# Layer 1's second half by pairs of tiles, with ScalarE's statistics and b1 added by transfers

## The chip, the cores and the metric

The kernel runs on one core of a Trainium2 chip. The metric is device time in microseconds (us) of one execution; lower is better. The engines work at the same time, each through its own queue in order: TensorE (PE: matmuls, with its weight loads as PEld), VectorE (DVE), ScalarE (ACT), GpSimd (POOL) and SyncE (SP). In this kernel POOL and SP issue the transfers (DMA).

## The reference, cut to what matters

Four graph layers follow each other on 2708 nodes with 512 features, all float32 and with the same dense adjacency matrix `adj`. Each layer normalizes x, keeps what is positive, and adds a graph convolution to x. The change is in the second layer, "layer 1":

```python
def _L1_gnn_ref(x, adj, W, b):
    deg = adj.sum(axis=1)
    dis = (deg + EPS) ** (-0.5)
    a_norm = dis[:, None] * adj * dis[None, :]
    h = a_norm @ x
    return h @ W.T + b

# --- layer 0 (adj_preln) ---
h = jnp.maximum(_layernorm(x, axis=-1), 0.0)
x = x + _L0_gnn_ref(h, adj, L0_gnn_weight)      # ends in relu, no bias
# --- layer 1 (adj_preln) ---
h = jnp.maximum(_layernorm(x, axis=-1), 0.0)
x = x + _L1_gnn_ref(h, adj, L1_gnn_W, L1_gnn_b)
# --- layers 2 and 3 in the same way; layer 3 is an attention layer with gates ---
```

`_layernorm` takes mean and variance over the 512 features of each node.

## The kernel before, in words

The 2708 nodes are kept as 20 full tiles of 128 nodes (0 to 19) and two tail tiles, 20 and 21, which hold the nodes left over in each quarter of the matrix. `h` is the normalized input of a layer and stays in SBUF. x itself lives in DRAM, one block of 128x512 a tile, named `xs0` to `xs21`.

A layer has two parts. The aggregation (`aggregate`, for layer 0 `first_aggregate`) multiplies `adj` with `h` by a scheme that needs seven block products in place of eight, twice nested: seven outer steps, each with two column pieces `u` of seven inner products. `multiply` writes one such piece: its products `pa`, `pb`, `pc`, `pd` are each five matmuls of 128x339 columns (L541), ScalarE copies `v` from `pa` (L575), and VectorE joins them (L581 makes `u2`, L588 `u3`, then L557 to L564 add to the sum `agg`). Before a piece, VectorE makes sums of matrix blocks (L512 to L516) that SP's transfers (L445, L447) brought into the seven places of `obuf`. A place becomes free again when the piece is done, so the transfers of a piece wait for the piece before.

The epilogue (`next_x`) multiplies `agg` with the layer's weight and makes the next x and h. It runs in two halves: the first (`H1`, tiles 0 to 9) after outer step 5, the second (`H2`, tiles 10 to 21) after outer step 3, the layer's last. For each tile: POOL loads the tile of x (L916), TensorE does four matmuls of 512 columns with the tile's columns of `agg` as weights (L203), VectorE scales the product and adds b1 (L931), adds it to x (L934), POOL stores x (L935), and VectorE takes mean and variance with bn_stats and bn_aggr (L234, L235). After three tiles, a chain of small instructions makes the scale and the shift (L239, ScalarE's square root L224, L225 to L230, L940, L247), and ScalarE writes the three tiles of `h` (L255). Tail tiles need their columns gathered first (L181), and tile 21 also takes two steps on TensorE (L206 and L210) with a copy by ScalarE between them (L208). In layers 0 and 2 ScalarE scales and cuts off the product (L929) in place of L931.

The same saving scheme with seven products exists for two tiles at once: `pair_product`, with `sums_of_pair` for the tiles and `weights_of_pairs` for the weight. Before, layer 3's gates use it (L1077 for its matmuls, of 257 columns), and layer 3's attention.

A scheduler orders the instructions of each engine: it follows the program's order, but moves ahead what it finds ready, so parts of neighbouring stages lie among each other. POOL's queue holds the loads and stores of x, the loads of the weights (`load_w`, L156) and the accumulating transfers of layer 0 (L744); a transfer that waits holds up those behind it.

Of the kernel before, what the change touches and what calls it, by code (L numbers as in the profile page):

```python
# [8 lines left out]
FP = mybir.dt.float32  # L9
AF = mybir.ActivationFunctionType  # L10
ALU = mybir.AluOpType

P = 128
D = 512
NC = D // P
# [3 lines left out]
KT = Q // P  # L19
# [3 lines left out]
W = (Q + 1) // U  # L23
NF = NQ * KT
# [13 lines left out]
def gnn_kernel(  # L38
# [20 lines left out]
    nc = tc.nc  # L59
# [5 lines left out]
    upool = ctx.enter_context(tc.tile_pool(name="upool", bufs=1))  # L65
    ytp = ctx.enter_context(tc.tile_pool(name="ytp", bufs=1))
    small = ctx.enter_context(tc.tile_pool(name="small", bufs=2))
    dram = ctx.enter_context(tc.tile_pool(name="dram", bufs=1, space=bass.MemoryType.DRAM))
    ps_agg = ctx.enter_context(tc.tile_pool(name="ps_agg", bufs=5, space=bass.MemoryType.PSUM))
# [23 lines left out]
    dinv = dd[:, 1]  # L93
# [52 lines left out]
    def take(places):  # L146

        places.append(places.pop(0))
        return places[-1]

    def new_y():
        return take(y_places)
# [6 lines left out]
    def full_cols(a, t):  # L159
        k = t % KT  # L160
        return a[..., k * P : (k + 1) * P]
# [75 lines left out]
    def rstd_of(mv, n):  # L237
        v = small_cols("rv", n)
        nc.vector.tensor_scalar(v[:, :n], mv[:, :n, 1], LN_EPS, None, ALU.add)  # L239
        rstd = small_cols("rstd", n)  # L240
        rsqrt(rstd[:, :n], v[:, :n], n)
        return rstd

    def shift_of(mv, scale, n, at=None):

        b = small_cols("sh", n)
        last = nc.vector.scalar_tensor_tensor(  # L247
            b[:, :n], mv[:, :n, 0], -1.0, scale[:, :n], ALU.mult, ALU.mult
        )
        if at is not None:  # L250
            at.append(last.ins)
        return b

    def normalized(t, src, scale, shift, fs=slice(0, D)):
        nc.scalar.activation(h[:, t, fs], src[:, fs], AF.Relu, bias=shift, scale=scale)  # L255
# [279 lines left out]
    def bank(name):  # L535
        return ps_agg.tile([P, W], FP, tag="agg", name=name)
# [131 lines left out]
    def aggregate(self_loops, epilogue, hooks=None):  # L668


        def outer(p, *dests):
            outer_product(p, self_loops, *dests)
            if hooks is not None and p in hooks:
                hooks[p]()

        outer(1, (0, 0, "as it is"))
        first_part_of_both()
        by_halves(nc.vector.tensor_sub, XA, XA, XB)
        outer(7, (1, 1, "as it is"))
        nc.vector.tensor_sub(XB, XB, XD)  # L680
        outer(2, (0, 0, "added"))
        minus_sum(XA, XD, XA)
        nc.vector.tensor_add(XC, XC, XA)
        outer(4, (1, 0, "as it is"))
        tails(self_loops, (0, 1))
        outer(6, (0, 1, "added"))
        ends_of_sums()
        outer(5, (0, 1, "less"), (1, 1, "less"))
        tails(self_loops, (2, 3))
        epilogue(H1)  # L690
        outer(3, (0, 1, "added"))
        epilogue(H2)
# [215 lines left out]
        epilogue(H2)  # L908


    def project(w_sb, t):
        return tile_product(t, tile_cols(agg, t), [w_sb[:, c, :] for c in range(NC)])

    def load_x(t, src):
        xt = take(xt_places)
        nc.gpsimd.dma_start(xt, src[t])  # L916
        return xt

    def next_x(ts, w_sb, scale, bias, src, colscale, after=None):
        for g in groups(ts):  # L920
            n, t0 = len(g), g[0]
            mv = small.tile([P, KT, 2], FP, tag="mv", name="mv")
            xts = []
            for s, t in enumerate(g):
                xt = load_x(t, src)
                po = project(w_sb, t)
                y = new_y()
                if bias is None:
                    nc.scalar.activation(y, po, AF.Relu, scale=scale[:, t : t + 1])  # L929
                else:  # L930
                    nc.vector.scalar_tensor_tensor(  # L931
                        y, po, scale[:, t : t + 1], bias, ALU.mult, ALU.add
                    )
                nc.vector.tensor_add(xt, xt, y)  # L934
                nc.gpsimd.dma_start(xs[t], xt)  # L935
                stats(xt, mv[:, s, :])
                xts.append(xt)
            rstd = rstd_of(mv, n)
            if colscale is not None:
                nc.vector.tensor_mul(rstd[:, :n], rstd[:, :n], colscale[:, t0 : t0 + n])  # L940
            sh = shift_of(mv, rstd, n)
            for s, t in enumerate(g):
                normalized(t, xts[s], rstd[:, s : s + 1], sh[:, s : s + 1])
                if after is not None:
                    after(t)
# [5 lines left out]
    w_sb = []  # L951

    def first_epilogue(ts):
        if not w_sb:
            w_sb.append(load_w(w0))
        next_x(ts, w_sb[0], dinv, None, x, dis)

    first_aggregate(first_epilogue)


    w1_sb = load_w(w1)
    b1_bc = misc[:, 0:D]
    nc.gpsimd.dma_start(b1_bc, b1.partition_broadcast(P))
    aggregate(False, lambda ts: next_x(ts, w1_sb, dis, b1_bc, xs, dinv))


    def broadcast_columns(po, cs):
# [54 lines left out]
    def make_vs():  # L1022
# [2 lines left out]

    aggregate(
        True,
        lambda ts: next_x(ts, w2_sb, dinv, None, xs, None, keep_h),
        {2: make_vs, 3: lambda: h_dots((5, 6))},
    )  # L1030

# [9 lines left out]
            wg_sb[:, :, k, D // 2 :], wab[0:D, k : k + 1].rearrange("(c p) o -> p c o", p=P)  # L1041
        )

    def in_four(a):
        return a.rearrange("p (k c o) -> p k c o", k=4, c=NC // 2)

    def weights_of_pairs(w, sums):

        w11, w12, w21, w22 = (w[:, f : f + 2, k] for f in (0, 2) for k in range(2))
        t1, t2, t3, t4 = sums
        nc.vector.tensor_sub(t1, w12, w11)
        nc.vector.tensor_sub(t2, w22, t1)
        nc.vector.tensor_sub(t3, w22, w12)
        nc.vector.tensor_sub(t4, w21, t2)
        return {1: w11, 2: w21, 3: w22, 4: t4, 5: t1, 6: t2, 7: t3}

    def sums_of_pair(ts, places):
        (a11, a12), (a21, a22) = (  # L1060
            [full_cols(agg[:, f, t // KT // 2, :, t // KT % 2], t) for f in range(2)] for t in ts
        )
        sums_ = take(places)
        s1, s2, s3, s4 = (sums_[:, k] for k in range(4))
        nc.vector.tensor_sub(s3, a11, a21)
        nc.vector.tensor_add(s1, a21, a22)
        nc.vector.tensor_sub(s2, a22, s3)
        nc.vector.tensor_sub(s4, a12, s2)
        return {1: a11, 2: a12, 3: s4, 4: a22, 5: s1, 6: s2, 7: s3}

    def pair_product(xs_, ws, bank, first_block_last=False):

        n = ws[1].shape[-1]

        def part(ps, k, start):
            for c in range(2):
                nc.tensor.matmul(  # L1077
                    ps, xs_[k][:, c], ws[k][:, c], start=start and c == 0, stop=c == 1,
                    skip_group_check=not start,
                )  # L1080

        def place(tag, bufs=1):
            return upool.tile([P, W], FP, tag=tag, name=tag, bufs=bufs)[:, 0:n]

        pa = bank("pa", n)
        part(pa, 1, True)
        v = place("v")
        nc.scalar.copy(v, pa)
        pb = bank("pb", n)
        part(pb, 6, True)  # L1090
        u2 = place("u2", 2)
        nc.vector.tensor_add(u2, v, pb)
        yield
        if not first_block_last:
            part(pa, 2, False)
        pc = bank("pc", n)
        part(pc, 7, True)
        u3 = place("u3")
        nc.vector.tensor_add(u3, u2, pc)
        yield  # L1100
        pd = bank("pd", n)
        part(pd, 5, True)
        c22 = place("s")
        nc.vector.tensor_add(c22, u3, pd)
        yield
        part(pc, 4, False)
        c21 = u3
        nc.vector.tensor_add(c21, u2, pc)
        part(pd, 3, False)
        c12 = u2  # L1110
        nc.vector.tensor_add(c12, u2, pd)
        if first_block_last:
            part(pa, 2, False)
        yield [[pa, c12], [c21, c22]]

    def gates_bank(name, n):
        pool, tag = (ps_out, "out") if name == "pb" else (ps_agg, "agg")
        return pool.tile([P, n], FP, tag=tag, name=name)

    both_places = ends[:, NC * D + 2 * NC :]  # L1120
    wg_sums = in_four(both_places[:, 0 : 4 * NC // 2 * GW])
    wg_sums = [wg_sums[:, k] for k in range(4)]
    s_places = [
        in_four(both_places[:, o : o + 4 * NC // 2 * P])
        for o in (4 * NC // 2 * GW, 4 * NC // 2 * (GW + P))
# [109 lines left out]
    def place(t):  # L1235

        if t < NF:
            o = (t // KT) * Q + (t % KT) * P
            return [(0, P, o)]
        if t == NF:  # L1240
            return [(q * R0, R0, q * Q + KT * P) for q in range(NQ)]
        return [(q * R1P + PAD, R1, q * Q + KT * P + R0) for q in range(NQ)]
# [231 lines left out]
```

## Time and profile before

| what | value |
| --- | --- |
| median of three runs | 2073.58 us (2071.27 to 2076.43) |
| the profiled execution, its own time | 2070.74 us |
| its span, first to last instruction | 2069.0 us, clock granted to TensorE 0.998 |
| VectorE, busy share | 72% |
| ScalarE, busy share | 20% |
| share of the chain of waits: TensorE, VectorE, DMA | 83%, 7%, 5% |
| layer 0's second epilogue, start on TensorE | 411.18 us |
| layer 1's first epilogue, start on TensorE | 717.36 us |
| layer 1's second epilogue, start on TensorE | 791.73 us |

A timeline line gives the start in us, the length, the engine, the line of the kernel, the operation with output and inputs, the shape and the number of instructions merged into it. One float32 matmul is two records. Records of matmuls overlap in the timeline, so what a matmul costs is read from one start to the next. In brackets stands the idle time ahead of the instruction and what ended it.

### The profile page before, as it was taken

The page shows a single profiled execution, that of the slowest core. Times are in us where ns is not written, and L with a number is a line of the kernel's source. Part 1 is how long each engine was busy: PE and PEld are TensorE (multiplying, and loading weights), DVE is VectorE, ACT ScalarE, POOL GpSimd, SP SyncE. Part 2 cuts the span into 40 slices and gives each one's busy share as a digit, 9 for nine tenths or more (in the row PEclk, how much of TensorE's full clock was granted, in tenths as well). Part 3 has the DMA queues.
Part 4 walks back from the last instruction along what each step waited for, and adds up shares of the span by engine and source line. Part 5 has one row for each costly group of instructions (what it writes and reads, how often), then busy time and mean ns, then how long its engine had stood idle before and what let it go on. Part 6 is the DMA issues. An engine that isn't in the chain of part 4 may idle for free.

```text
span 2069.0 us, 20285 instructions
## 1 busy us (share of the span) xinstructions
PE 2028.0 (98%) x7330; PEld 1282.2 (62%) x7330; DVE 1495.6 (72%) x2592; ACT 406.2 (20%) x822; POOL 198.8 (10%) x361
## 2 busy tenths in 40 slices
PE   5999999999999999999999999999999999999998
PEld 2566655646666655666664646666677666676666
DVE  4678877756777777766587889967758866677644
ACT  1430001130000010100002130000026444444411
POOL 0111111120000011100002130001001000001011
PEclk9999999999999999999999999999999999999999
DMA  9998595555545444754454565545543332323231
GB/s 369 305 378 265 180 338 187 190 186 179 174 154 176 146 168 142 239 178 161 161 170 144 204 208 188 171 156 186 185 147 121 112 105 95 110 88 123 87 100 52
DMA packets 81476, 363.69 MB, mean 176 GB/s; under 512 B 11568, under 2 KB 16876, under 8 KB 81248
## 3 DMA queue, kind: packets, MB, share of 16 engines
q1 hardware_dynamic: 51104, 245.95, 34.7%
q0 software_dynamic: 30272, 116.45, 17.4%
q8 instruction: 58, 0.95, 0.2%
q14 instruction: 42, 0.34, 0.0%
HBM read 297.39 MB, written 62.19 MB: 174 GB/s over the span
## 4 chain that ended last, share of the span: by engine, by line
PE 83%; DVE 7%; DMA 5%; issue 4%; POOL 1%; ACT 0%; SPq 0%; POOLq 0%; DVEq 0%; ACTq 0%
PE pe L1364 17%; PE pc L541 13%; PE pa L541 13%; PE pd L541 13%; PE po L203 8%; PE pb L541 7%; PE pt L603 3%; DMA obuf<-in_yb_dram 3%; PE pd L1077 1%; PE pc L1077 1%; PE pa L1077 1%; PE pt L608 1%; PE pe L603 1%; DMA osumt<-ends 1%; DVE ends L1004 1%
## 5 line engine op out<-in xcount | busy, mean ns | idle before, releaser
L1364 PE MATMUL pe<-obuf,h 128*128 128x339 f32 x1280 | 373.2, 448 | 0.0
L541 PE MATMUL pa<-obuf,h 128*128 128x339 f32 x1040 | 317.0, 449 | 2.5 <-ACT h L255 1.4
L1364 PEld LDWEIGHTS pe<-obuf,h 128*128 128x128 f32 x1280 | 241.4, 189 | 121.8 <-issue 4.1
L541 PEld LDWEIGHTS pa<-obuf,h 128*128 128x128 f32 x1040 | 195.2, 189 | 109.5 <-issue 9.2
L203 PE MATMUL po<-ends,agg 128*128 128x512 f32 x480 | 207.5, 593 | 0.0
L1228 ACT ACTIVATE e<-r,nsr 128x339 f32<-128x339 f32 x352 | 172.4, 566 | 178.5 <-DVE obuf L1232 86.4
L541 PE MATMUL pb<-t,s 128*128 128x339 f32 x560 | 170.9, 451 | 1.8 <-DVE s L473 1.0
L541 PE MATMUL pc<-t,h 128*128 128x339 f32 x560 | 169.5, 448 | 1.5 <-DVE u L588 1.5
L541 PE MATMUL pd<-t,s 128*128 128x339 f32 x560 | 169.0, 447 | 0.0
L541 PE MATMUL pd<-obuf,s 128*128 128x339 f32 x550 | 166.3, 448 | 0.2 <-DVE agg L562 0.2
L575 ACT COPY v<-pa 128x339 f32<-128x339 f32 x56 | 24.6, 439 | 718.2 <-PE pa L541 691.3
L203 PEld LDWEIGHTS po<-ends,agg 128*128 128x128 f32 x480 | 90.9, 190 | 114.3 <-issue 109.3
L541 PEld LDWEIGHTS pb<-t,s 128*128 128x128 f32 x560 | 106.3, 191 | 57.3 <-DVE t L513 2.1
L541 PEld LDWEIGHTS pc<-t,h 128*128 128x128 f32 x560 | 105.7, 189 | 56.8 <-DVE u L588 3.1
L541 PEld LDWEIGHTS pd<-t,s 128*128 128x128 f32 x560 | 105.8, 189 | 54.1
L541 PEld LDWEIGHTS pd<-obuf,s 128*128 128x128 f32 x550 | 104.0, 189 | 53.9 <-DVE agg L562 1.3
L541 PE MATMUL pc<-obuf,s 128*128 128x339 f32 x450 | 135.9, 448 | 0.0
L541 PEld LDWEIGHTS pc<-obuf,s 128*128 128x128 f32 x450 | 85.1, 189 | 43.8 <-issue 0.5
L935 POOL DMA_DIRECT2D xs<-ends x66 | 35.9, 544 | 780.6 <-DVE ends L934 705.4
L513 DVE TENSOR_TENSOR t<-obuf,t 128x1695 f32<-128x1695 f32 x55 | 105.3, 1915 | 0.0
L1232 DVE SCALAR_TENSOR_TENSOR obuf<-obuf,e 128x1695 f32<-128x1695 f32 x32 | 61.5, 1923 | 57.9 <-DMA obuf<-in_yb_dram 40.7
L514 DVE TENSOR_TENSOR t<-obuf,t 128x1695 f32<-128x1695 f32 x52 | 99.5, 1914 | 0.1
(321 smaller groups left out, 2415.4 us busy)
## 6 DMA issues: line engine op xcount, KB each, us to landing
obuf<-in_yb_dram SPq DMA_DIRECT2D x132, 847.5 KB, 4.5
obuf<-osumt SPq DMA_DIRECT2D x100, 847.5 KB, 4.5
osumt<-obuf POOLq DMA_DIRECT2D x22, 847.5 KB, 12.2
xs<-ends POOLq DMA_DIRECT2D x66, 256.0 KB, 2.3
ends<-xs POOLq DMA_DIRECT2D x60, 256.0 KB, 4.2
obuf<-in_yt_dram SPq DMA_DIRECT2D x28, 339.0 KB, 3.6
obuf<-in_yb_dram POOLq DMA_DIRECT2D x11, 847.5 KB, 11.0
ends<-in_yb_dram SPq DMA_DIRECT2D x9, 847.5 KB, 9.2
```

Of the source, the lines that this page charges most:

```text
L203: nc.tensor.matmul(po, cs[c], ws[c], start=(c == 0), stop=(c == NC - 1))
L513: nc.vector.tensor_add(t2, o22, t1)
L514: at_y.append(nc.vector.tensor_add(t4, o21, t2).ins)
L541: last = nc.tensor.matmul(ps, x[:, k, :], y[:, k, :], start=start and k == 0, stop=k == KT - 1, skip_group_check=not start,)
L575: at_v.append(nc.scalar.copy(v, pa).ins)
L603: nc.tensor.matmul(ps[c], h[:, NF, c * P : (c + 1) * P], tl[:, 0, :], start=start, stop=False)
L608: nc.tensor.matmul(ps[c], h[g, NF + 1, c * P : (c + 1) * P], tl[g, 1, :], start=False, stop=True)
L935: nc.gpsimd.dma_start(xs[t], xt)
L1077: nc.tensor.matmul(ps, xs_[k][:, c], ws[k][:, c], start=start and c == 0, stop=c == 1, skip_group_check=not start,)
L1228: nc.scalar.activation(e[:, k], row, AF.Exp, bias=nsr[:, t, s : s + 1], scale=1.0)
L1232: nc.vector.scalar_tensor_tensor(b, b, 0.0, e1[:, :n], ALU.not_equal, ALU.min)
L1364: nc.tensor.matmul(pe[c], h[:, t, c * P : (c + 1) * P], a, start=(t == 0), stop=False)
```

## The change

1. In layer 1 alone, the second half (tiles 10 to 21) is done by `next_x_by_pairs`: first the tail tiles 20 and 21 as before by `next_x`, then tiles 10 to 19 as five pairs by `pair_product`, each with seven products of two matmuls of 256 columns.
2. In those pairs, mean and variance come from ScalarE (`stats_by_act`): a sum, a scaling, a sum of squared differences and another scaling, in place of bn_stats and bn_aggr.
3. b1 is no longer added in the epilogue. While layer 0 and layer 1 run, 22 accumulating transfers on POOL's queue add it to the kept x in DRAM, one a tile (`add_b1`). They are handed over after outer steps 7, 2, 4 and 6 of layer 1; the scheduler may place them earlier, and in the built order they stand among layer 0's stores of x. In layer 1 the scaled product is added to x in one VectorE instruction, in both halves.
4. The pairs need room: the sums of the weight take two quarters of `misc` (where b1 lay) and part of one of the seven places of `obuf`, which is borrowed until the last pair is done; the sums of the tiles take the tail tile's place `yt` and the rest of that block. The sums of the weight are ready to run once w1 is loaded, and in the built order the first two stand on VectorE near the start of layer 1.

The functions for pairs move ahead of `next_x` in the file without other change, but that `in_four` now returns a list. Layers 0, 2 and 3 compute what they did.

```diff
+    def places_of_pairs():
+        blk = free.pop(0)
+        flat = blk.rearrange("p k w -> p (k w)")
+        yt_ = ytp.tile([P, 2, W], FP, tag="yt", name="sp").rearrange("p s w -> p (s w)")
+        return (
+            [a[:, k * D : (k + 1) * D] for a in (misc, flat) for k in range(2)],
+            [a[:, k * 2 * P : (k + 1) * 2 * P] for a in (yt_, flat[:, 2 * D :]) for k in range(2)],
+            blk,
+        )
+
+    def stats_by_act(xt, mv):
+        y = new_y()
+        nc.scalar.activation(y, xt, AF.Identity, accum_out=mv[:, 0:1])
+        nc.scalar.activation(mv[:, 0:1], mv[:, 0:1], AF.Copy, scale=1.0 / D)
+        nc.scalar.activation(y, xt, AF.Square, bias=mv[:, 0:1], scale=-1.0, accum_out=mv[:, 1:2])
+        nc.scalar.activation(mv[:, 1:2], mv[:, 1:2], AF.Copy, scale=1.0 / D)
+
+    def next_x_by_pairs(ts, w_sb, scale, relu, src, colscale, after=None):
+        next_x([t for t in ts if t >= NF], w_sb, scale, relu, src, colscale, after)
+        w_places, s_place, blk = places_of_pairs()
...
+        ws = weights_of_pairs(
+            w_sb.rearrange("p c (k o) -> p c k o", k=2),
+            [a.rearrange("p (c o) -> p c o", c=NC // 2) for a in w_places],
+        )
+        halves = [slice(k * (D // 2), (k + 1) * (D // 2)) for k in range(2)]
+        pairs = [(t, t + 1) for t in ts if t < NF][::2]
+        xs_ = sums_of_pair(pairs[0], s_places)
+        for n, pair in enumerate(pairs):
+            xts = [load_x(t, src) for t in pair]
+            mv = small.tile([P, KT, 2], FP, tag="mv", name="mv")
+            *_, po = pair_product(xs_, ws, gates_bank)
+            if n + 1 < len(pairs):
+                xs_ = sums_of_pair(pairs[n + 1], s_places)
+            for s, (t, xt) in enumerate(zip(pair, xts)):
...
+                        nc.vector.scalar_tensor_tensor(
+                            xt[:, f], c, scale[:, t : t + 1], xt[:, f], ALU.mult, ALU.add
+                        )
...
+                nc.gpsimd.dma_start(xs[t], xt)
+                stats_by_act(xt, mv[:, s, :])
+            rstd = rstd_of(mv, 2)
...
+            sh = shift_of(mv, rstd, 2)
+            for s, (t, xt) in enumerate(zip(pair, xts)):
+                normalized(t, xt, rstd[:, s : s + 1], sh[:, s : s + 1])
...
+        free.append(blk)

     def next_x(ts, w_sb, scale, relu, src, colscale, after=None):
...
-                    nc.vector.scalar_tensor_tensor(
-                        y, po, scale[:, t : t + 1], bias, ALU.mult, ALU.add
-                    )
-                nc.vector.tensor_add(xt, xt, y)
+                    nc.vector.scalar_tensor_tensor(
+                        xt, po, scale[:, t : t + 1], xt, ALU.mult, ALU.add
+                    )
...
     w1_sb = load_w(w1)
-    b1_bc = misc[:, 0:D]
-    nc.gpsimd.dma_start(b1_bc, b1.partition_broadcast(P))
-    aggregate(False, lambda ts: next_x(ts, w1_sb, dis, b1_bc, xs, dinv))
+    def add_b1(ts):
+        for t in ts:
+            nc.gpsimd.dma_start(xs[t], b1.partition_broadcast(P), accum_op=ALU.add)
+
+    aggregate(
+        False,
+        lambda ts: (next_x if ts[0] < half else next_x_by_pairs)(
+            ts, w1_sb, dis, False, xs, dinv
+        ),
+        {p: lambda k=k: add_b1((H1 + H2)[k * 6 : k * 6 + 6]) for k, p in enumerate((7, 2, 4, 6))},
+    )
```

In the changed file, the pair's functions stand at these lines: the sums of the weight L920 to L924, the sums of a pair L932 to L935, a pair's matmuls L944, its copy `v` L955, its joins L959 to L978, the scaled add L1039, ScalarE's statistics L1010 to L1013, the accumulating transfers L1103; `next_x`'s rstd times `colscale` is L1077 there, and in the pairs L1048.

## The prediction

> **What bounds the kernel now.** The page's busy times come first, then the chain of waits and the timelines around the two places that the change touches.
>
> ```profile
> PE 2028.0 (98%) x7330; PEld 1282.2 (62%) x7330; DVE 1495.6 (72%) x2592; ACT 406.2 (20%) x822; POOL 198.8 (10%) x361
> ```
>
> TensorE is busy for 2028.0 of 2069.0 us, so time is won only by taking work from it or by closing one of its gaps, and anything that makes it wait is paid in full. The TensorE timeline (start, length, engine, line, what, count of records) shows the stretch that the change rewrites, the second epilogue of layer 1:
>
> ```profile
> 791.73 34.49 PE L203 MATMUL po<-ends,agg 128*128 128x512 f32 x80
> 826.06 3.60 PE L203 MATMUL po<-ends 128*128 128x512 f32 x8
> 829.59 1.06 PE L206 MATMUL po<-ends 128*32 128x512 f32 x6
> 835.57 3.02 PE L541 MATMUL pb<-t,s 128*128 128x339 f32 x10
> 838.43 3.02 PE L541 MATMUL pa<-obuf,h 128*128 128x339 f32 x10
> 848.01 2.27 PE L541 MATMUL pc<-t,h 128*128 128x339 f32 x7 [0.85 <-DVE u L588]
> ```
>
> Call the start, 791.73, T. Ten full tiles take 34.33 us up to 826.06 (3.43 each), tail tile 20 takes 3.53, and from 829.59 tail tile 21 shares TensorE with layer 2's first product until 835.57. The product after that starts at T + 46.70, and at 848.01 there is one real gap, 0.85 us. The same weight form as the new one stands in layer 3's gates:
>
> ```profile
> 1501.86 1.03 PE L1077 MATMUL pa<-ends,agg 128*128 128x257 f32 x4
> 1502.73 1.03 PE L1077 MATMUL pb<-ends 128*128 128x257 f32 x4
> 1503.60 1.03 PE L1077 MATMUL pa<-ends,agg 128*128 128x257 f32 x4
> ```
>
> A product of a pair starts 0.867 us after the last one; seven make 6.07 us for two tiles, where two plain tiles take 6.87.
>
> **The change, part by part.** The sum is made against the profiled execution (2070.74 us, span 2069.0 and 1.74 around it); the median of the runs, 2073.58, lies 2.84 higher, and I carry the difference over to it.
>
> *TensorE's own work.* Five pairs: 5 x 6.07 = 30.35 for 34.33, 3.98 us less. Tail 21 alone, from the same lines in layer 0 (start to start), is 1.32 (L206, 449.04 to 450.36) + 0.85 (L210); with the first product of layer 2 (2.86) that makes 5.03, where 829.59 to 835.57 is 5.98. So 0.95 of gap goes when the tails move to the front and lie among pair products. The stage becomes 30.35 + 3.53 + 2.17 = 36.05 us, and two products on (5.72) TensorE would be at T + 41.8 in place of T + 46.7: 4.9 us won. The 0.85 at 848.01 goes too if later work comes late anyway. Together 5.8 us, were nothing given back.
>
> *VectorE in the stage.* A pair brings 4 sums (L932 to L935), 5 joins (L959 to L978) and 4 scaled adds (L1039), all 128x256: they start 0.33 us apart in the gates' rows (1493.20, 1493.54), so 4.3 us, and seven small ones of the rstd chain at 0.20 (805.34, 805.53) 1.4: 5.7 us against TensorE's 6.07. It fits, barely, with no room for waits. bn_stats and bn_aggr (0.72 and 0.20 a tile) and the add of b1 (0.72) leave VectorE in this half, and one of two 128x512 adds leaves in the first half too; TensorE waits for none of these there now, so they are worth nothing by themselves. The first pair's sums are queued before the last product of outer step 3, so TensorE can start on a pair at T; what is behind are tail 21's two scalings and statistics, which now stand between a pair's joins: 0.6 us (bounds 0 and 1.5, two 0.75 operations).
>
> *ScalarE.* Its statistics have rows in layer 0:
>
> ```profile
> 81.02 0.63 ACT L291 ACTIVATE y<-h 128x512 f32<-128x512 f32 x1
> 81.55 0.19 ACT L291 ACTIVATION_READ_ACCUMULATOR y<-h 128x1 f32 x1
> 97.75 0.73 ACT L286 ACTIVATE y<-h,mv 128x512 f32<-128x512 f32 x1
> 98.39 0.18 ACT L286 ACTIVATION_READ_ACCUMULATOR y<-h,mv 128x1 f32 x1
> 828.34 2.22 ACT L255 ACTIVATE h<-ends,sh,rstd 128x512 f32<-128x512 f32 x3 [2.58 <-DVE sh L247]
> ```
>
> A sum is 0.755 from start to start, a sum of squares 0.91, and each is followed by a small scaling of 0.2: 2.07 us a tile; a normalization (L255) is 0.74. These instructions run in order in one queue with the copies `v` (L955, 0.36) that TensorE needs before it may add to the same bank, and with layer 2's first copy (L575, 0.44). In the built order ten normalizations, nine tiles' statistics and the tenth's first two instructions, three pair copies and four roots stand before that L575 from the tails' normalization on. The tails' shift is queued on VectorE behind pair 1's last join, which reads TensorE's product at T + 14.8 (four products 3.47, tails 5.70, then 6.5 products); ScalarE starts at T + 15.6. 7.4 + 18.6 + 1.0 + 1.1 + 0.8 + 0.44 = 29.3 us, so L575 ends at T + 44.9. If each of a tile's four instructions waits for the one before as the small VectorE ones do (0.16 long, 0.20 apart), add 0.05 x 4 x 9.5 = 1.9: T + 46.8. I take the middle, T + 45.9, so TensorE's next product starts at T + 46.0. Part of that shows earlier, at pair 4's copy (queued behind four tiles' statistics and two normalizations, due at about T + 27.4 and ready near T + 28.7). The stage thus wins 46.7 - 46.0 = 0.7, not 4.9; the 0.6 of VectorE lies inside. Bounds: 4.9 won if ScalarE keeps ahead; 3.3 lost (T + 50) if it idles 4 us more for VectorE's results.
>
> Against switching among root, square and identity on ScalarE speaks a table load, but the trace has only three (1.28 us each, at 11.4, 41.1 and 1429.4 us), and L224's roots, L286's squares and L291's sums run between 80 and 126 us with none, so I put nothing. The Trainium skill ("ScalarE: Activation LUTs", What ACT_TABLE_LOAD costs) puts about 2.66 us on every switch to another set; by that, two switches in each of five pairs would be an estimated 27 us, and the sum would end near 2100.
>
> *b1 by transfers.* 22 accumulating transfers of 256 KB go on POOL's queue among layer 0's stores and loads. The trace has none into DRAM. Nearest: 847.5 KB accumulated (L744) lands after 11.4 us (7.2 to 15.9); scaled by size that is 3.4, and 11.4 is the upper bound. Each waits for its tile's store to land (2.3 median, 8.2 at worst) and holds the queue. In layer 0 that meets loads of x made seven places ahead (two tiles, 6.9 us, to spare), so nothing there. The Trainium skill ("DMA: Bandwidth & Descriptors", Anatomy of one DMA, SWDGE path) has 2.0 us plus bytes over 436e3, an estimated 2.6 us for 256 KB; for 847.5 KB it gives 4.0 where the row shows 11.4, so the row decides.
>
> *The load of w1* is where the queue counts. The sums of w1 (L920, L921) stand on VectorE ahead of layer 1's first joins, and wait for it. The lines are from POOL's timeline, the list of transfers between 450 and 462 (last number: us from issue to landing) and VectorE's timeline.
>
> ```profile
> 450.73 0.76 POOL L156 DMA_DIRECT2D ends<-in_w_dram  x1 [0.89 <-PE po L206]
> ends<-in_w_dram POOLq DMA_DIRECT2D x1, 1024.0 KB, 8.4
> 464.48 0.50 DVE L588 TENSOR_TENSOR u<-u,pc 128x339 f32<-128x339 f32 x1
> ```
>
> Now w1 lands at 450.73 + 8.4 = 459.1. Behind it will stand L920 0.72, L1077 0.2, L921 0.72, L247 0.2, L581 0.43, L512 1.85, L516 1.85, L588 0.5: 6.5 us, so L588 ends at 465.6, exactly when TensorE wants it (its next product starts at 465.60). The load itself goes later: store of tile 18 issued by 445.6 and landed at 448.7 (3.1 us, the median of the five stores between 820 and 850), its accumulate until 449.5, store 19 until 450.1, three loads at 0.70 until 452.2: 1.5 us later. So 1.5 us of new gap (bounds 0, and 6.6 if that store lands after 8.2).
>
> *No price.* One block lent to the pairs returns after the last product; the load into it and the next one then compete (8.0 us for the next before), but ScalarE's delay covers 1 to 2 us. A tail load moved behind it (0.34 MB) is not needed before layer 3's end.
>
> Sum: -0.7 (stage) - 0.85 (gap at 848) + 1.5 (w1) = -0.05 us. **Forecast: 2073.5 us**, no change; TensorE's saving is handed to ScalarE's queue and to w1.
>
> **Rivals.**
> *A. The pairs run clean*, as layer 3's gates do (five pairs in 31 us, 1489.4 to 1520.4). For: those rows, VectorE's 5.7 under 6.07. Against: no statistics and no roots stand there. -5.8: 2067.8.
> *B. VectorE and ScalarE in lockstep* (slower). VectorE's rv and reciprocal wait for ScalarE's statistics and root, ahead of the next pair's joins; ScalarE's next sum waits for VectorE. If a pair's statistics end after the following pair's pc product (about 4 us after its last product), each of five pairs costs 2 us more: T + 41.8 + 10 = T + 51.8, 5.1 lost, with w1's 1.5: 2080.2. For: four tiles' statistics before pair 4's copy. Against: two pairs of slack in the built order.
> *C. POOL's queue* (slower): accumulates land as late as 11.4 us and stores at 8.2, w1 costs 6.6, the rest as forecast: -1.55 + 6.6 = +5.0, 2078.6. For: the DMA engines are 90% busy from 450 us on. Against: 3.4 us by size.
>
> **How the numbers follow.** Forecast 0.46, A 0.20, B 0.18, C 0.16. A measurement here tells about 0.3% (6.2 us) from no change. A reaches that only with runs at its lucky end: faster 0.06. Slower takes half of B and C and a little of the forecast's upper end: 0.20. Same 0.74. From A less 1 to just over B: 2067 to 2081.
>
> **What would show it.** L944 products 0.867 apart and 36 to 40 us for the stage; ScalarE busy through it with L1010 and L1012, and TensorE waiting for L955 and L575; a wait before layer 1's L588 with w1 as its end; no new table load. TensorE without waits there makes it A; VectorE idle for ScalarE at L239 and L225 with TensorE waiting at L966 makes it B; accumulates landing over 8 us make it C. Any gap outside these two places makes the sum wrong.

## The result, and the profile after

The changed kernel is slower: 2099.51 us (median of 4 runs, 2094.67 to 2102.21) against 2072.43 (4 runs beside it), a ratio of 1.0125 with a 95% interval of 1.0101 to 1.0149. The forecast of no change and its range (up to 2081) are both wrong. The profiled execution of after took 2102.21 us, its span is 2100.4; the one of before has a span of 2069.0. Medians here and below are of executions at the usual clock; one of `layer0_tails_last` (2142.78 us, granted clock 0.948) is left out.

The page of the changed kernel, engines first, then the group whose idle time grew most (busy us and mean ns | idle us ahead of it and what ended it; for the same group before, the idle time was 1.5):

```profile
PE 2033.5 (97%) x7390; PEld 1300.0 (62%) x7390; DVE 1492.3 (71%) x2625; ACT 425.2 (20%) x889; POOL 218.6 (10%) x382
L541 PE MATMUL pc<-t,h 128*128 128x339 f32 x560 | 172.3, 454 | 16.1 <-DVE u L588 16.1
```

TensorE's busy time even rose, though the pairs ask less work of it; why is seen below. Its timeline shows where the time was lost, and where some was won (the matmuls in the stretch of the pairs); after first, then the lines of before for the stretch around layer 1's start:

```profile
381.82 4.63 PE L541 MATMUL pa<-obuf,h 128*128 128x339 f32 x10 [2.10 <-ACT v L575]
...
417.90 34.50 PE L203 MATMUL po<-ends,agg 128*128 128x512 f32 x80
452.23 3.60 PE L203 MATMUL po<-ends 128*128 128x512 f32 x8
455.76 1.41 PE L206 MATMUL po<-ends 128*32 128x512 f32 x8
457.10 1.41 PE L541 MATMUL pa<-obuf,h 128*128 128x339 f32 x4
463.17 2.07 PE L210 MATMUL po<-ends,all_again 128*128 128x512 f32 x2 [4.66 <-ACT ends L208]
465.04 3.60 PE L541 MATMUL pa<-obuf,h 128*128 128x339 f32 x6
468.43 3.11 PE L541 MATMUL pb<-t,s 128*128 128x339 f32 x10
...
477.09 3.02 PE L541 MATMUL pd<-t,s 128*128 128x339 f32 x10
493.96 5.76 PE L541 MATMUL pc<-t,h 128*128 128x339 f32 x10 [13.85 <-DVE u L588]
499.55 3.02 PE L541 MATMUL pd<-obuf,s 128*128 128x339 f32 x10
...
824.08 1.02 PE L944 MATMUL pa<-ends,agg 128*128 128x256 f32 x4
...
860.31 3.02 PE L541 MATMUL pa<-obuf,h 128*128 128x339 f32 x10
...
876.22 3.12 PE L541 MATMUL pc<-t,h 128*128 128x339 f32 x10 [1.09 <-DVE u L588]
```

```profile
449.04 1.39 PE L206 MATMUL po<-ends 128*32 128x512 f32 x8
...
454.18 3.02 PE L541 MATMUL pb<-t,s 128*128 128x339 f32 x10
...
465.60 3.02 PE L541 MATMUL pc<-t,h 128*128 128x339 f32 x10
468.46 3.02 PE L541 MATMUL pd<-obuf,s 128*128 128x339 f32 x10
```

The loss lies 330 us ahead of the pairs, in layer 0's epilogues and at the start of layer 1. From start to start on TensorE, in us:

| stretch | before | after | more |
| --- | --- | --- | --- |
| start to layer 0's first epilogue | 336.49 | 339.15 | 2.66 |
| from there to layer 0's second epilogue | 74.69 | 78.75 | 4.06 |
| from there to the product after layer 1's first pc | 57.28 | 81.65 | 24.37 |
| from there to layer 1's second epilogue | 323.27 | 324.53 | 1.26 |
| from there to layer 2's first pc (the pairs) | 56.28 | 52.14 | -4.14 |
| from there to the end | 1220.99 | 1224.18 | 3.19 |

The pairs win 4.14; the two stretches in which the transfers of b1 stand lose 28.4. The first row looks like chance: its code is unchanged, and in the runs below it ends anywhere from 337.3 to 342.0; the one profile of before has the lowest value. Of the last row, 3.0 is what one gap in layer 3, in unchanged code, and the product behind it grew by.

What happened shows on POOL's timeline in layer 0's second epilogue (in brackets the idle time ahead and what ended it; L1072 is the store of x, L1103 the accumulate):

```profile
425.87 0.88 POOL L1103 DMA_DIRECT2D xs<-in_b_dram  x1 [2.08 <-DMA xs<-ends]
426.68 0.67 POOL L1072 DMA_DIRECT2D xs<-ends  x1
431.22 0.87 POOL L1103 DMA_DIRECT2D xs<-in_b_dram  x1 [3.88 <-DMA xs<-ends]
431.79 0.88 POOL L1072 DMA_DIRECT2D xs<-ends  x1
436.62 0.85 POOL L1103 DMA_DIRECT2D xs<-in_b_dram  x1 [3.95 <-DMA xs<-ends]
437.19 0.87 POOL L1072 DMA_DIRECT2D xs<-ends  x1
437.74 1.94 POOL L993 DMA_DIRECT2D ends<-in_x_dram  x3
442.50 0.89 POOL L1103 DMA_DIRECT2D xs<-in_b_dram  x1 [2.82 <-DMA xs<-ends]
```

Each accumulate waits at the head of the queue until the store just issued has landed. Only then does the next tile's store go out, although VectorE finished that tile earlier, by more with every tile. A tile takes 5.4 to 5.9 us in this queue and 3.43 on TensorE, so the queue falls behind a little more with every tile, and the loads of x and of w1 stand in it too. VectorE waited 6.51 us for such a load of x until 374.09 and 5.68 until 461.75, ScalarE waited for VectorE, and TensorE for ScalarE (the 2.10 and 4.66 above). The view of POOL's waits from 336 to 500 us (total, times, longest):

```profile
POOL xs L1103 <- DMA xs<-ends: 78.2, 17, 9.4
```

The lists of transfers from 340 to 500 us (last number: median us from issue to landing), after and then before:

```profile
xs<-ends POOLq DMA_DIRECT2D x22, 256.0 KB, 5.9
xs<-in_b_dram POOLq DMA_DIRECT2D x22, 256.0 KB, 6.0
...
ends<-in_w_dram POOLq DMA_DIRECT2D x1, 1024.0 KB, 13.9
```

```profile
xs<-ends POOLq DMA_DIRECT2D x22, 256.0 KB, 2.3
...
ends<-in_w_dram POOLq DMA_DIRECT2D x1, 1024.0 KB, 8.4
```

A store takes 5.9 in place of 2.3. w1 is issued at 473.88 (before: 450.73) and lands after 13.9, at 487.8. VectorE's timeline shows the end of that chain:

```profile
487.78 0.69 DVE L920 TENSOR_TENSOR ends<-ends 128x512 f32<-128x512 f32 x1 [17.56 <-DMA ends<-in_w_dram]
...
493.40 0.50 DVE L588 TENSOR_TENSOR u<-u,pc 128x339 f32<-128x339 f32 x1
```

And each long gap costs more than itself. By stretch (busy time of each engine, then the granted clock, the DMA share, GB/s):

```profile
480.00:494.00 14.00, 0.15 (x2) 0.05 (x1) 6.09 (x8) 2.55 (x4) 3.36 (x5) 0.58 0.86 243
494.00:500.00 6.00, 6.00 (x12) 3.75 (x13) 3.15 (x6) 0.00 (x0) 0.00 (x0) 0.56 0.53 148
500.00:520.00 20.00, 20.00 (x72) 13.24 (x71) 13.27 (x18) 0.88 (x2) 0.00 (x0) 1.00 0.51 175
```

After 13.85 us of idling TensorE works at 0.56 of its clock: the ten matmuls of pc take 5.59 us in place of 2.86. That, with the slower products after the other gaps, is the higher busy time.

### The profile page after: what moved, and what is told of

The parts are those of the page before. It is cut to its first block, busy times and chain, and to the rows that moved or that the text cites. A ratio compares the mean times of both kernels' runs of the same rounds, so it can differ in the third digit from the quotient of the medians.

```text
span 2100.4 us, 20535 instructions
## 1 busy us (share of the span) xinstructions
PE 2033.5 (97%) x7390; PEld 1300.0 (62%) x7390; DVE 1492.3 (71%) x2625; ACT 425.2 (20%) x889; POOL 218.6 (10%) x382
## 3 DMA queue, kind: packets, MB, share of 16 engines
q0 software_dynamic: 33360, 121.95, 19.3%
## 4 chain that ended last, share of the span: by engine, by line
PE 73%; issue 11%; DVE 6%; DMA 6%; POOL 2%; ACT 0%; SPq 0%; POOLq 0%; DVEq 0%; ACTq 0%
PE pe L1434 17%; PE pa L541 12%; PE pc L541 12%; PE pd L541 12%; PE pb L541 6%; PE po L203 5%; PE pt L603 3%; DMA obuf<-in_yb_dram 3%; PE pa L944 1%; PE pd L944 1%; PE pc L944 1%; DMA ends<-in_yt_dram 1%; PE pt L608 1%; DMA xs<-ends 1%; PE pe L603 1%
## 5 line engine op out<-in xcount | busy, mean ns | idle before, releaser
L541 PE MATMUL pa<-obuf,h 128*128 128x339 f32 x1040 | 321.6, 454 | 4.7 <-ACT v L575 3.2
L203 PE MATMUL po<-ends,agg 128*128 128x512 f32 x400 | 173.1, 593 | 0.0
L575 ACT COPY v<-pa 128x339 f32<-128x339 f32 x56 | 24.7, 441 | 716.0 <-PE pa L541 676.6
L203 PEld LDWEIGHTS po<-ends,agg 128*128 128x128 f32 x400 | 75.7, 190 | 95.4 <-issue 92.1
L1072 POOL DMA_DIRECT2D xs<-ends x56 | 36.6, 692 | 690.6 <-DVE ends L1067 323.2
L513 DVE TENSOR_TENSOR t<-obuf,t 128x1695 f32<-128x1695 f32 x55 | 105.4, 1916 | 0.1
L581 DVE TENSOR_TENSOR u<-v,pb 128x339 f32<-128x339 f32 x56 | 28.3, 505 | 101.5 <-PE pb L541 99.1
## 6 DMA issues: line engine op xcount, KB each, us to landing
obuf<-in_yb_dram POOLq DMA_DIRECT2D x11, 847.5 KB, 10.7
```

What stands on the lines that cost most here:

```text
L203: nc.tensor.matmul(po, cs[c], ws[c], start=(c == 0), stop=(c == NC - 1))
L513: nc.vector.tensor_add(t2, o22, t1)
L541: last = nc.tensor.matmul(ps, x[:, k, :], y[:, k, :], start=start and k == 0, stop=k == KT - 1, skip_group_check=not start,)
L575: at_v.append(nc.scalar.copy(v, pa).ins)
L581: at_u2.append(nc.vector.tensor_add(u2, v, pb).ins)
```

## The experiments

Ratios are against the kernel before, run on the same chip beside each run; differences in us are between medians, each with its own few us of scatter.

### Is it the transfers, and which place of theirs?

`b1_behind_w1` holds the accumulates behind the load of w1, `pairs_no_b1` leaves them out (and b1 with them), `b1_alone` is the kernel before with them, `sums_late` keeps them and moves VectorE's sums of w1.

```diff
 pairs_no_b1, in the call of aggregate for layer 1:
-        {p: lambda k=k: add_b1((H1 + H2)[k * 6 : k * 6 + 6]) for k, p in enumerate((7, 2, 4, 6))},
 b1_alone, in the kernel before, for layer 1:
-                        y, po, scale[:, t : t + 1], bias, ALU.mult, ALU.add
+                        xt, po, scale[:, t : t + 1], xt, ALU.mult, ALU.add
                     )
-                nc.vector.tensor_add(xt, xt, y)
+                if bias is None:
+                    nc.vector.tensor_add(xt, xt, y)
...
+        {p: lambda k=k: add_b1((H1 + H2)[k * 6 : k * 6 + 6]) for k, p in enumerate((7, 2, 4, 6))},
 b1_behind_w1:
     def add_b1(ts):
+        with tc.issue_after(at_w[-1]):
+            for t in ts:
+                nc.gpsimd.dma_start(xs[t], b1.partition_broadcast(P), accum_op=ALU.add)
 sums_late:
+        with tc.issue_after(at_end[-24]):
+            ws = weights_of_pairs(
...
```

> The changed kernel, but the 22 accumulating transfers of b1 stand on POOL's queue behind layer 0's last stores and the load of w1; nothing else moves. Theory Q (the queue): in layer 0 each accumulate waits for its own tile's store to land and holds up the next store, the loads of x and the load of w1; the three gaps this makes on TensorE cost 3.9 + 7.5 + 16.8 = 28.2 us, while the pairs win about 4.1. Then this kernel ends near 2099.5 - 28.2 = 2071 or, counted from before, 2072.4 - 4.1 = 2068; I expect 2066 to 2072, and no wait of L588 over 2 us before layer 1's first pc. Rival P (the traffic): 22 accumulates of 256 KB slow the transfers beside them wherever they stand, now the first blocks of layer 1: 2080 or more, with TensorE waiting for blocks between 460 and 560 us. Rival S (the pairs): the loss comes from the sums of w1, the borrowed block or ScalarE: 2095 or more.

> The changed kernel without the accumulating transfers; b1 is left out of the result. Theory Q and rival P both expect before less the pairs' gain: 2072.4 - 4.1 = 2068 (2066 to 2071). Rival S expects 2075 or more. Against the run with the transfers behind w1 it prices these there: Q 0 to 2 us, P 10 or more.

> The kernel before, with b1 added by the same 22 accumulating transfers at the same places of POOL's queue and the scaled add of the changed kernel, but without pairs: full tiles by next_x in both halves, bn_stats, no sums of w1. Theory Q: the gaps at layer 0's first half (3.9) and at its tail (7.5) stay, the wait for w1 (16.8) goes since no sum of w1 stands on VectorE before layer 1's first joins: 2072.4 + 11.4 = 2084 (2080 to 2088). Rival P: the traffic costs 20 us or more by itself: 2092 or more. Rival S: 2072 to 2075.

> The changed kernel, but the sums of w1 (L920 to L924) are held on VectorE behind a join late in layer 1. Theory Q: the wait of 13.85 us for w1, and the slower product after it (2.7), go: 2099.5 - 16.8 = 2083 (2079 to 2087). Rival R: something else of the late queue stands there next (tile 21's store, the first blocks), so that TensorE still waits 5 us or more before layer 1's first pc: 2088 or more.

| run | median us | ratio (95%) |
| --- | --- | --- |
| b1_behind_w1 | 2093.31 | 1.0102 (1.0087 to 1.0117) |
| pairs_no_b1 | 2070.54 | 0.9989 (0.9980 to 0.9998) |
| b1_alone | 2090.94 | 1.0092 (1.0077 to 1.0107) |
| sums_late | 2084.20 | 1.0062 (1.0044 to 1.0080) |

Rival S falls: without the transfers (and without b1 in layer 1's first half too) the pairs are 2.4 us faster than before, and with the transfers alone the old kernel is 18 us slower. `sums_late` came out as theory Q said (2083): of the loss, 15.3 us is VectorE waiting for w1. But Q alone falls too. Behind w1 no store and no load of layer 0 is held up, and 20 of the 27 us are still lost; `b1_alone` lost 7 more than Q's 11.4, of which 5.9 is a wait of 4.21 us at 514 for VectorE, which waits for a block there, and the slower product behind it. TensorE's timeline of `b1_behind_w1` says where:

```profile
496.48 5.25 PE L543 MATMUL pc<-t,h 128*128 128x339 f32 x10 [6.79 <-DVE u L590]
509.11 3.12 PE L543 MATMUL pb<-t,s 128*128 128x339 f32 x10 [1.66 <-DVE s L475]
528.11 4.80 PE L543 MATMUL pc<-t,h 128*128 128x339 f32 x10 [7.30 <-DVE u L590]
```

In VectorE's timeline these are waits for layer 1's blocks (10.04, 4.23 and 9.55 us for transfers into `obuf`), beside which the accumulates run from 459 to 515. In that stretch the blocks from `osumt` land after 15.2 us (median), in the kernel before after 4.4, and the DMA share is 0.92 in place of 0.55. From the pages, the queue of POOL's transfers took 19.3% of 2100.4 us of all 16 engines after and 17.4% of 2069.0 before: 45 us more, about 2 for each accumulate of 256 KB. So rival P has its part: the bytes cost where they meet the block loads.

### Waiting or traffic?

`lag3` keeps the transfers in layer 0 but queues each behind the store of three tiles later (at the end, behind the last store). `b1_spread` puts three behind each column piece of layer 1, `b1_quiet` moves these from the piece's last join to its first.

```diff
 lag3:
+            with tc.issue_after(stores[min(t + 3, 21)]):
                 nc.gpsimd.dma_start(xs[t], b1.partition_broadcast(P), accum_op=ALU.add)
 b1_spread (in outer_product, after multiply):
+            at = nc.gpsimd.tensor_copy(seen, agg[:, fh, ih, 1, 0, u * W : u * W + 1]).ins
+            for _ in range(min(3, len(b1_todo))):
+                with tc.issue_after(at):
+                    t = b1_todo.pop(0)
+                    nc.gpsimd.dma_start(xs[t], b1.partition_broadcast(P), accum_op=ALU.add)
 b1_quiet, against b1_spread:
-            at = nc.gpsimd.tensor_copy(seen, agg[:, fh, ih, 1, 0, u * W : u * W + 1]).ins
+            at = nc.gpsimd.tensor_copy(seen, agg[:, fh, ih, 1, 1, u * W : u * W + 1]).ins
```

> The changed kernel, but each accumulate is queued on POOL behind the store of the tile three places later, so the store it needs has landed by then; the same 22 transfers of the same size in the same stretch of layer 0. Theory Q (waiting in the queue is what costs in layer 0): stores, loads of x and w1 are issued on time and the time falls to 2071 to 2077. Theory P (the traffic: by the queue's own share of time the 22 accumulates take 45 us of all 16 DMA engines, 2.06 us each): loads and w1 still land late beside them, 2080 or more.

> The changed kernel with the accumulates really spread: three of them behind each column piece of layer 1's outer steps 7, 2, 4 and 6, held there by a copy of one column on POOL that reads the piece's last sum. Q and P both expect the loss to go, since neither the queue nor the DMA engines (share 0.5) are short there: 2070.5 as without the transfers, 2069 to 2073. If every accumulate beside a block load costs as it did behind w1 (23 us for 22 there), 2080 or more.

> The spread kernel with one thing moved: the three accumulates of a piece are held behind the piece's first join (after pd) in place of its last. In the kernel before, SP's block loads fill the DMA engines from the end of a piece for some 14 us (share 0.7 to 0.95 in stretches of 2 us) and leave 4 to 6 us idle ahead of its end, which is where these then start. Theory P2 (the transfers cost only where they meet SP's just-in-time loads): the waits of L600, 2 to 4.7 us a piece, shrink to under 1 us and the time falls from 2109.5 to 2071 to 2085 (six of 6.2 us in a window of 4 to 6 may spill). If the place in the piece does not matter, 2105 or more.

`lag3`: 2079.61, ratio 1.0036 (1.0023 to 1.0048). Taking the waits away, with the same bytes in the same stretch, wins back 20 of 27 us, so the waiting is the larger part in layer 0. It is still 9 us above the kernel without b1: w1 lands after 12.1 us, and TensorE waits 3.72 for L588 and then works slowly through pc (5.69 from start to start). `b1_spread`: 2109.52, ratio 1.0179 (1.0165 to 1.0192), the opposite of what both theories expected. TensorE waits in each of the seven pieces that have three accumulates beside them (the last single one brings no wait); two of the seven:

```profile
544.85 4.53 PE L553 MATMUL pc<-t,h 128*128 128x339 f32 x10 [2.97 <-DVE u L600]
570.53 4.81 PE L553 MATMUL pc<-t,h 128*128 128x339 f32 x10 [4.01 <-DVE u L600]
```

The mean DMA share of 0.5 had misled me. In the kernel before, one piece by stretches (DMA share and GB/s are the last two numbers):

```profile
572.00:580.00 8.00, 8.00 (x30) 5.30 (x29) 7.50 (x14) 0.44 (x1) 0.00 (x0) 1.00 0.68 226
580.00:586.00 6.00, 6.00 (x23) 3.97 (x22) 2.79 (x4) 0.44 (x1) 0.00 (x0) 1.00 0.72 220
586.00:592.00 6.00, 6.00 (x23) 3.98 (x22) 4.97 (x5) 0.00 (x0) 0.00 (x0) 1.00 0.00 0
592.00:600.00 8.00, 8.00 (x30) 5.30 (x29) 2.02 (x6) 0.44 (x1) 0.00 (x0) 1.00 0.65 219
```

The blocks come in bursts that begin when a piece frees its places, and are needed as soon as they land; then the DMA engines lie idle for some 6 us. `b1_spread` set its transfers off at the start of the burst: seven waits, 23.3 us, and a slower product after each. `b1_quiet`, started in the idle stretch, took 2094.29 (ratio 1.0112, 1.0092 to 1.0132): 15 us better from the place within the piece alone, less than I expected. Three accumulates do not fit into it: they land after 9.2 us (median), and in the piece after those issued from 494 the DMA share is 0.92 to 0.98. One at a time was not tried. The Trainium skill ("DMA: Bandwidth & Descriptors", Issuing engines are not separate DMA queues) says that transfers from all issuing engines run interleaved on the same 16 DMA engines; these runs agree: accumulates from POOL's queue made SP's block loads land late (15.2 us in place of 4.4 above).

### b1 without transfers

`b1_pool` lets GpSimd add b1 to the loaded x of the pairs, and VectorE in the other tiles as before; `pool_tails_last` and `pool_both_halves` vary the pairs (the second has the tails last too, and so have `layer0_both_halves` and `both_three_places`). `b1_layer0` adds b1 on VectorE in layer 0, before the store, and the rest build on it.

```diff
 b1_pool (in next_x_by_pairs):
+            for xt in xts:
+                nc.gpsimd.tensor_add(xt, xt, bias)
 b1_layer0 (in next_x, layer 0 alone):
-                nc.gpsimd.dma_start(xs[t], xt)
                 stats(xt, mv[:, s, :])
+                if keep_plus is not None:
+                    nc.vector.tensor_add(y, xt, keep_plus)
+                    nc.gpsimd.dma_start(xs[t], y)
+                else:
+                    nc.gpsimd.dma_start(xs[t], xt)
 layer0_tails_last, spread_tails_last, pool_tails_last: next_x for the tails after the pairs
 layer0_bn_stats, spread_bn_stats: stats(xt, mv[:, s, :]) for stats_by_act(xt, mv[:, s, :])
 both_three_places, against layer0_both_halves:
+    third_y = misc[:, D : 2 * D]
+    y_places.append(third_y)
...
```

> The changed kernel without accumulating transfers: in the pairs GpSimd adds b1 to the loaded tile of x (ten additions of 128x512), in the first half and the tails VectorE adds it as in the kernel before; b1 lies in one of the seven places for x. If GpSimd keeps ahead of the pairs it equals the kernel without b1: 2069 to 2072. If an addition waits for a load on POOL's queue and holds the stores and the next loads, as the accumulates did in layer 0, the pairs' stage gets longer than 52.4 us and TensorE waits there: 2074 to 2085.

> The same with the tail tiles behind the pairs. From the spread runs (51.5 us from the first pair product to layer 2's first pc, against 52.9): 1 us less than with the tails in front, 2068 to 2071. By my prediction's sum, 0.95 more.

> The same with pairs in both halves of layer 1. TensorE's own work falls by another 3.98 us: 2064 to 2068 if the first half runs as clean as the second. Against it: the borrowed block is taken while SP loads for outer step 3, and ten more additions stand on POOL's queue among loads and stores: 2072 to 2080 then.

> The changed kernel with no extra transfer at all: in layer 0's epilogue VectorE adds b1 to the new x after its statistics, and that sum is what is stored (22 additions of 128x512, 0.72 us each, into the place of the scaled product). If bytes and waits of the accumulates are the whole loss, this equals the kernel without b1, 2069 to 2072, though b1 is there. If VectorE has no room in layer 0's epilogues (it is busy some 2 of 3.4 us a tile there), TensorE waits for it at layer 0's tail or at layer 1's first pc: 2074 to 2080.

> The kernel with b1 added in layer 0 and the tails last, with pairs in both halves of layer 1. TensorE's own work falls by another 3.98 us. If the first half runs as clean as the second: 2064 to 2068. If the borrowed block, taken while outer step 3's blocks are due, or VectorE, which there also makes outer step 3's first sums, makes TensorE wait: 2070 to 2078.

> The kernel with b1 added in layer 0, pairs in both halves of layer 1 and the tails last, with a third place for the scaled products of layer 0. In the run with two places a product (L1066) and the tail's gather (L181) wait for a store to land before they may write the place it reads: 1.2 us and 0.25 in the first half, 5.27 and a slower product (1.9) at the tail. If that is what is left of b1's cost, 2071.6 falls to 2063 to 2069 and is faster than both kernels. If it is not the places, 2070 to 2073.

| run | median us | ratio (95%) |
| --- | --- | --- |
| b1_pool | 2079.90 | 1.0040 (1.0025 to 1.0055) |
| pool_tails_last | 2078.59 | 1.0029 (1.0016 to 1.0043) |
| pool_both_halves | 2083.98 | 1.0061 (1.0045 to 1.0076) |
| b1_layer0 | 2075.54 | 1.0011 (1.0002 to 1.0020) |
| layer0_both_halves | 2071.62 | 0.9988 (0.9979 to 0.9997) |
| both_three_places | 2068.22 | 0.9979 (0.9969 to 0.9990) |

GpSimd's addition takes 1.27 us, but it waits on POOL's queue for the load of x and stands in the pairs' path (from 797 to 850 the additions wait 4.3 us for loads, and VectorE 4.0 for the additions): the same fault as the accumulates'. In layer 0 VectorE has the room, and all but 2.4 of the 27 us are gone (it is 5.0 above `pairs_no_b1`); the waits that stayed in layer 0 were for a place that a store was still reading (TensorE waits 1.19, 0.25 and 0.64 us behind L1066 and L181). With a third place and pairs in both halves the kernel beats both: by 0.2%, 5.2 us under the kernel before, about 31 under the changed one.

### ScalarE or VectorE, and the tails

> The spread kernel with bn_stats and bn_aggr on VectorE in the pairs in place of ScalarE's statistics. If ScalarE's queue held the stage, as I had it, this wins or costs nothing against the spread kernel (-3 to +1). If VectorE is the tight one (5.7 us a pair plus 1.84 makes 7.5 over TensorE's 6.07), five pairs cost 5 to 7 us more. If neither is tight, within 1 us.

> The kernel with b1 added in layer 0, and bn_stats and bn_aggr on VectorE in the pairs. My prediction had ScalarE's statistics as what holds the stage (4 us): then this wins up to 4 us. In the spread kernel the stage grew by 8.5 us with VectorE's statistics, beside other disturbances; if VectorE is the tight engine (5.7 us a pair plus 1.84, against TensorE's 6.07), 5 to 9 us more than with ScalarE's.

> The spread kernel with the tail tiles behind the pairs, as before. By my sum the tails in front save the 0.95 of gap at tile 21: +1 us here (0 to 3). The rival is that the last pair's statistics and normalization at the end of the stage are what comes late, and then the tails behind them give cover: -2 to 0.

> The same with layer 1's tail tiles behind the pairs. In the spread runs this made the way from the first pair product to layer 2's first pc 1.3 us shorter (51.5 against 52.9), with GpSimd's additions 3 us; I expect 0.5 to 2 us less than with the tails in front: 2068 to 2071. By my prediction's sum it would be 0.95 more.

bn_stats in place of ScalarE's statistics costs 10.1 us against `b1_spread` (`spread_bn_stats` 2119.59, ratio 1.0226, 1.0205 to 1.0248) and 9.4 against `b1_layer0` (`layer0_bn_stats` 2084.90, ratio 1.0053, 1.0040 to 1.0067). From `layer0_bn_stats`, two lines of TensorE's timeline and one of VectorE's:

```profile
830.30 1.13 PE L944 MATMUL pa<-ends,agg 128*128 128x256 f32 x4 [0.69 <-ACT v L955]
860.30 5.70 PE L541 MATMUL pc<-t,h 128*128 128x339 f32 x10 [8.54 <-DVE u L588]
857.29 0.69 DVE L1139 CUSTOM_DVE_ANT_0 ends<-ends 128x512 f32<-128x512 f32 x1 [6.89 <-DMA ends<-in_wsa_dram]
```

The price is only in part VectorE's work. The pairs with the tails take 1.8 us longer there (from the first L944 to layer 2's pb, less one product of 2.86: 38.0 in place of 36.2). Most of the rest is the wait of 8.54 us and the slow product behind it, and in 6.89 of it VectorE stands idle: an instruction of layer 3's preparation (L1139) is ahead of L516 and L588 in its order in this build and waits for a load. In `b1_layer0` the instruction that stands there (846.66) finds its load landed. `spread_bn_stats` has the same wait (6.87). So ScalarE's statistics make the faster kernel as built, but how much of the 9.4 us is the statistics and how much the order, no run separates. The tails behind the pairs were better in all three couples: by 1.6 (`spread_tails_last` 2107.94, ratio 1.0175, 1.0155 to 1.0195), 1.3 (with GpSimd) and 1.9 us (`layer0_tails_last` 2073.61, ratio 1.0002, 0.9992 to 1.0012). In each the intervals overlap; the sign is the same in all.

## Why the prediction was wrong, step by step

- **The step that failed: b1 by transfers.** I priced one accumulate (3.4 us) and one store (2.3) by themselves and wrote that the queue "meets loads of x made seven places ahead (two tiles, 6.9 us, to spare), so nothing there". The queue is a chain: store, landing, accumulate, next store. It takes 5.4 to 5.9 us a tile against TensorE's 3.43, and twelve tiles use up 6.9 us of slack after three or four. The sentence ahead of it, that each accumulate waits for its tile's store to land and holds the queue, was right; the multiplication by the number of tiles was missing. In place of 0 it cost 4.1 in the first epilogue and 7.5 at the tail (from L206 to layer 1's first pb 12.67, before 5.14). `lag3` shows it as waiting: with the same bytes and almost no such waits, 20 of the 27 us come back, here and at w1.
- **The load of w1.** The mechanism was right (L920 ahead of layer 1's joins), the size was not: 1.5 us forecast, upper bound 6.6, measured 16.8 (13.85 of waiting and a slower product, from the start of pd at 477.09 to 499.55, before 5.7). The bound took the last store alone as late, and not the queue's backlog: w1 went out 23.2 us later than before. `sums_late`, without the wait for w1, is 15.3 us faster.
- **Rival C came nearest**, as a loss in POOL's queue, but 21 us too cheap, and its own sign did not show: it had accumulates landing over 8 us, and they landed after 6.0 (median; one at 11.8 was the longest). What it lacked is the same chain. The traffic I did not see at all: I had bounded landing times, and not the time that 22 transfers take from others' loads.
- **TensorE in the pairs: right.** The stage took 36.23 us (824.08 to 860.31); I had 36.05.
- **ScalarE: wrong by 3.7 us, on the other side.** I had L575 end at T + 45.9, it ended at T + 42.2. Its instructions were a little shorter than their rows (a tile's four in 1.95 us in place of 2.07, a pair of normalizations in 1.42), its copies and roots came closer together too, and the 0.95 us (half of 1.9) that I added for each waiting on the last did not come. From T to layer 2's first pc the stage won 4.14, where I had 0.7 and the gap of 0.85. That gap did not go: it is 1.09 at 876.22.
- **VectorE at 5.7 us a pair: not contradicted.** TensorE's timeline has no wait for a join within the stage. With bn_stats and bn_aggr, 1.84 a pair more, the stage grew by 1.8 us.
- **Tails in front**: 0.95 forecast as a gain; the runs lean to a loss of 1.3 to 1.9.
- **No table load: right.** There are three as before, at 0.74, 31.05 and 1446.31. The times in the prediction are some 10.7 us late against the span (before: 0.74, 30.45 and 1418.75); nothing rests on them. The Trainium skill's price for a switch ("ScalarE: Activation LUTs", What ACT_TABLE_LOAD costs) led to a sum near 2100; the time lies there by chance, from another cause.
- **The chances**: 0.20 for slower. The cases differed in what ScalarE and w1 do; none let the loss in layer 0 grow tile by tile.

Open: of what is left of `lag3` (9 us), 6.6 is the wait for w1 and the slow pc behind it; the rest is not placed. How much of the queue's slowness is waiting and how much traffic within layer 0 is known only as far as `lag3` goes.

## What to carry to other kernels

An instruction put into a queue that runs once a tile has to be priced as that queue's time per tile, with its waits, against the pace of the engine that sets the time; slack of two tiles is nothing against a deficit that adds up. A mean DMA share of 0.5 may be a burst of loads that are needed just in time followed by idle engines, so look at it in stretches of a few us before placing transfers there. The small addition was cheapest here on an engine with time to spare at the moment when the data was already in its hands (VectorE in layer 0, before the store).

## What the runs showed of the hardware

- After some gaps TensorE works at a lower granted clock for some us (0.56 from 494 to 500 in after): gaps of 1.90 us (`b1_quiet`), 2.00 and 4.01 (`b1_spread`), 2.10 and 13.85 (after) were followed by a product of 4.4 to 5.6 us in place of 2.86, so each cost 1.6 to 2.7 us above itself. Gaps of 2.16 (`b1_alone`), 2.33 (`sums_late`) and 3.22 (`b1_quiet`) were not. The Trainium skill ("TensorE: Matmul & The Clock Gate", Part 1) puts the fall to half the clock after an idle window of about 3.4 us that runs freely; here it came after less than two thirds of that, and no run shows what decides between these gaps.
- An accumulating transfer of 256 KB into DRAM takes some 1.8 to 2.3 us of all 16 DMA engines (POOL's queue in after, `b1_behind_w1`, `b1_spread`, `lag3` and `b1_quiet` against `pairs_no_b1`, 17.2% of 2071.4 us), and landed after 6.0 us (median) beside the stores.
